# A two-layer graph network on one core: separate banks for two products, a range check kept per batch, a norm's sum from VectorE, and new orders

## The chip, the cores and the metric

The kernel runs on one core of a Trainium2 chip. The core has five engines with a queue each: TensorE (PE in the profile, with its weight loads shown apart as PEld) multiplies matrices, VectorE (DVE), ScalarE (ACT) and GpSimd (POOL) work on elements, and SyncE (SP) issues DMAs. TensorE writes into PSUM, which has eight banks here (`"ps": 8`); everything else lives in SBUF or in DRAM. An engine runs its queue in order; waits between engines go over semaphores. The metric is the device time of one execution in microseconds, the median of several runs; lower is better.

## The reference

`x` has 64 batches of 256 tokens with 512 features. Each batch goes through two layers, both with the same 256 x 256 adjacency `adj`, and each layer ends in a residual and a layer norm.

```python
# layer 0: attention with 8 heads of 64, masked by adj
q, k, v = x @ Wq + bq, x @ Wk + bk, x @ Wv + bv          # split into heads
scores = einsum('bqhd,bkhd->bhqk', q, k) / sqrt(64) + (1 - adj) * -1e9
x = layernorm(x + einsum('bhqk,bkhd->bqhd', softmax(scores), v) @ Wo + bo)
# layer 1: attention with one head from two scalars per token
h = x @ W
e = leaky_relu((h @ a1)[:, :, None] + (h @ a2)[:, None, :], 0.2) * adj
x = layernorm(x + elu(softmax(e) @ h + beta * h))
```

## The kernel before

**Products.** Every large product of layer 0 and layer 1 is done by a scheme of seven products in place of eight (`project`, L436): both factors are cut into quarters, sums of quarters are made beforehand (`weight_sums`, `streamed`, `token_sums`), and seven products of quarters are added up to the four quarters of the result. Product 1, 6 and 7 accumulate in one bank (`ps_chain`), 5 and 3 in another (`ps_cross`); between them their values are read out: `copy` starts a quarter of the result, `add` adds to it. Product 2 and 4 are the second and the fourth. Where the result is 256 wide (q, k, v, done for two batches at once) they have banks of their own (`ps_second`, `ps_fourth`); where it is 128 wide (`width == P`: spread, o, u) they share the two halves of one bank (`ps_pair`), and product 4 is recorded with `[second]` as something that it waits for (L480). ScalarE copies and VectorE adds (`gather`, L487); for o, VectorE adds all parts into X (L943).

**Stages of a pair of batches.** The kernel takes the batches two by two (`pair`, L616). "x" brings the pair in transposed; "q", "k" and "v" project it. Then for each batch (0 or 1, the digit behind a stage's name): "scores" in four calls of two heads, with keys on the partitions (matmuls of tile shape 64*128, two at a time); VectorE adds the mask (L783), ScalarE takes the exponential (L785), GpSimd adds the two halves (L788), VectorE transposes and reduces them to partial sums (L794, L795). "sums" folds these with one small matmul into `ps_den` (128*64), VectorE takes the reciprocal `inv` (L806), and two steps of DMA spread it over the partitions (L810, L814). "mix" multiplies the exponentials with v (`ps_pv`, 128*64); ScalarE copies, VectorE multiplies by the spread reciprocals (L867). "o" projects onto the residual X. `norm` (L581) then takes the sum of a token on ScalarE (L588, first pass), the mean on VectorE (L594), the squares on ScalarE (L588, second pass), the inverse root on GpSimd (L599 to L601), and scales on ScalarE (L605). "logits" and "attention" make layer 1's softmax from two scalars per token (L968) and two round trips over DRAM; "spread" multiplies it with X (`yT`), "u" multiplies by W. `finish` (L712) takes the exponential on ScalarE (L716), adds the positive part and then the rest on VectorE (L717, L719), calls `norm` again and stores.

**Order.** No engine's order is written by hand except TensorE's, in outline. `ROUND` lists the stages of one round; `LATER` says how many rounds after its own pair a stage is done, so that a round holds stages of several pairs; `FINISH` lists the closing stages. `Plan` (L62) records all operations with estimated durations and places them: TensorE in the order of the turns, the last 70 turns freely (`OPEN`), the other engines by due times worked back from TensorE, and with the slots of each pool as limits. In a round of before, TensorE does v, spread1, o1, q, u1, sums0, mix0, the scores of one batch, k, spread0, o0, u0, sums1, mix1 and the scores of the other batch (x, logits and attention have no matmul here).

**The range check.** The fast path is right if all reciprocals of the softmax sums lie between 1e-15 and 1e15. They are all kept in a DRAM tile `rows_all`; at the end it is read back (L1121) and compared as a whole (`check`, L1125). For the last batch `last_ok` does it apart. If the check fails, the program does everything again in a slower, general way.

Of the kernel before, what the change touches and what calls it, by code (L numbers as in the profile page):

```python
# [12 lines left out]
ALU = mybir.AluOpType  # L13
AX = mybir.AxisListType
PSUM = bass.MemoryType.PSUM

P = 128
# [2 lines left out]
ALPHA = 0.2  # L20
NEG = -1000000000.0

ROUND = ("scores20", "x", "scores10", "v", "logits0", "spread1", "o1", "q", "u1", "sums0", "mix0", "scores11",
         "scores01", "attention0", "attention1", "scores31", "scores21", "k", "logits1", "spread0", "o0", "u0",
         "sums1", "mix1", "scores00", "scores30")

LATER = {"mix1": 0, "sums1": 0, "scores30": -1, "scores20": 0, "scores00": -1, "scores10": 0, "logits0": 1, "v": 0,
         "spread1": 2, "o1": 1, "u1": 2, "x": -1, "mix0": 0, "sums0": 0, "scores31": 0, "scores21": 0, "scores01": 0,
         "scores11": 0, "attention0": 1, "q": -1, "attention1": 1, "logits1": 1, "k": -1, "spread0": 1, "o0": 0, "u0":
         1}  # L30

FINISH = (("logits0", 1), ("attention0", 1), ("scores20", 0), ("v", 0), ("spread1", 2), ("scores10", 0), ("o1", 1),
          ("scores21", 0), ("sums0", 0), ("u1", 2), ("mix0", 0), ("logits1", 1), ("attention1", 1), ("spread0", 1),
          ("u0", 1), ("scores11", 0), ("scores31", 0), ("o0", 0), ("u1", 1), ("sums1", 0), ("attention1", 0),
          ("attention0", 0), ("logits0", 0), ("spread1", 1), ("mix1", 0), ("o1", 0), ("u0", 0), ("logits1", 0),
          ("scores01", 0), ("u1", 0), ("spread1", 0), ("spread0", 0))
SAFE = 1e15


# [204 lines left out]
def gnn_two_layers(ctx: ExitStack, tc: tile.TileContext, x, adj, Wq, bq, Wk, bk, Wv, bv, Wo, bo, W, a, beta, out):  # L244
# [11 lines left out]


    slots = {"xin": 2, "x": 4, "two": 6, "xP": 1, "piece": 6, "full": 4, "half": 17, "flip": 1, "part": 1, "inv": 1,
             "xS": 2, "st": 76, "ps": 8, "rows": 4, "svT": 4, "line": 4, "square": 4}

    class Pool:

# [18 lines left out]
    def st(n, name):  # L281
        return sb("st", [n], name)
# [57 lines left out]
    ones = const.tile([P, 48], F32, name="ones")  # L340
    nc.gpsimd.memset(ones, 0.0)
    nc.gpsimd.memset(ones[:, 16:32], 1.0)
    rows_all = Buf(dram_pool, "rows_all", [B - 1, H * N], "rows_all")
    slots["rows_all"] = plan.slots["rows_all"] = 1
    stay.append(rows_all)
    last_ok = st(1, "last_ok")
    fold_sb = once([32], "fold_sb")
    plan.op("DVE", 150, lambda: nc.vector.tensor_reduce(
# [87 lines left out]
    def project(left, right, by_feature, claims, copy, add, inner=2, width=P, first=False):  # L436

        shape = [2, width] if by_feature else [width // P, F]
        chain, cross = ps(shape, "ps_chain"), ps(shape, "ps_cross")
        if width == P:
            both = ps([2] + shape, "ps_pair")
            second, fourth = (both, 0), (both, 1)
        else:
            second, fourth = (ps(shape, "ps_second"), None), (ps(shape, "ps_fourth"), None)

        def product(n, dst, start):  # L450
            l, r = sides[n][0](), right[n - 1][0]()
            for f in range(2 if by_feature else width // P):
                for c in range(inner):
                    lhs, rhs = (l[:, c, blk(f)], r[:, c, :]) if by_feature else (r[:, c, blk(f)], l[:, c, :])
                    nc.tensor.matmul(dst[:, f, :], lhs, rhs, start=start and f == 0 and c == 0, stop=c == inner - 1,  # L455
                                     skip_group_check=True)

        ns = 224 * inner * 2 if by_feature and width == P else 432 * inner * (width // P)

        sides = {}  # L460

        def pe(n, to, start, after=()):
            buf, part = to
            acc = (lambda: buf[A]) if part is None else (lambda: buf[:, part])
            sides[n] = left(n) if callable(left) else left[n - 1]
            plan.op("PE", ns, lambda: product(n, acc(), start), sides[n][1] + right[n - 1][1] + list(after),
                    [to] + list(after), claims=claims)
            return to, acc

        chain, cross = (chain, None), (cross, None)  # L470
        copy((0, 0), pe(1, chain, True))
        if first:
            add((0, 0), pe(2, second, True))
        copy((1, 1), pe(5, cross, True))
        if not first:
            add((0, 0), pe(2, second, True))
        copy((0, 1), pe(6, chain, False))
        if not first:
            add((0, 1), pe(3, cross, False))
        copy((1, 0), pe(4, fourth, True) if second[1] is None else pe(4, fourth, False, [second]))  # L480
        if first:
            add((0, 1), pe(3, cross, False))
        acc = pe(7, chain, False)
        add((1, 1), acc)
        add((1, 0), acc)
# [92 lines left out]
    for sv in spare:  # L578
        plan.op("POOL", 100, lambda sv=sv: nc.gpsimd.memset(sv[A], 0.0), [], [sv])

    def norm(X, ts):  # L581

        n = len(ts)
        sums, mean, sq, rs, nm = (st(n, name) for name in ("sum", "mean", "sq", "rs", "nmr"))

        def total(i, t, func, to, bias):
            junk = sb("half", [D], "junk")
# [1 line left out]
                junk[A], X[:, t, :], func, bias=mean[:, i:i + 1] if bias else 0.0, accum_out=to[:, i:i + 1]),  # L589
                [(X, (t, 0)), (X, (t, 1))] + ([mean] if bias else []), [junk, (to, i)])  # L590

        for i, t in enumerate(ts):
            total(i, t, AF.Identity, sums, False)
        plan.op("DVE", 170, lambda: nc.vector.tensor_scalar(mean[A], sums[A], -1.0 / D, None, ALU.mult), [sums], [mean])  # L594
        for i, t in enumerate(ts):
# [103 lines left out]
    def batch(m, s, qT, kT, V, dram, general):  # L699
# [11 lines left out]

        def finish(ts, us, u, mode):  # L712

            for t in ts:
                m = sb("half", [D], "m")
                plan.op("ACT", 620, lambda t=t, m=m: nc.scalar.activation(m[A], u(t), AF.Exp), us(t), [m])  # L716
                plan.op("DVE", 685, lambda t=t: nc.vector.scalar_tensor_tensor(  # L717
                    X[:, t, :], u(t), 0.0, X[:, t, :], op0=ALU.max, op1=ALU.add), us(t), tokens(t), mode=mode)
                plan.op("DVE", 685, lambda t=t, m=m: nc.vector.scalar_tensor_tensor(  # L719
                    X[:, t, :], m[A], 1.0, X[:, t, :], op0=ALU.min, op1=ALU.add), [m], tokens(t), mode="two")  # L720
            norm(X, ts)
            for t in ts:
                plan.op("SP", 455, lambda t=t: nc.sync.dma_start(dram(out, s)[:, t, :], X[:, t, :]), tokens(t), [],
                        lag=2300)
# [35 lines left out]
        def attention_by_keys():  # L760
# [38 lines left out]
            def denominators():  # L799

                turn("sums")
                acc, inv = ps([32], "ps_den"), sb("inv", [32], "inv")
                plan.op("PE", 80, lambda: nc.tensor.matmul(  # L803
                    acc[0:P // 2], part[A].rearrange("p h q -> p (h q)"), fold_sb[A], start=True,
                    stop=True), [part, fold_sb], [acc], mode="one", claims=[inv])
                plan.op("DVE", 342, lambda: nc.vector.reciprocal(inv[0:P // 2], acc[0:P // 2]), [acc], [inv])  # L806
                spread_rows(lambda r: r.rearrange("(p q) -> p q", q=32), lambda: inv[0:H * N // 32], inv)

            def spread_rows(to, src, inv):
                plan.op("SP", 540, lambda: nc.sync.dma_start(to(rows_all[b]), src()), [inv], [(rows_all, b)], lag=1700)  # L810
                for i in range(2):
                    def spread(i=i):
                        r = rows_all[b]
                        nc.sync.dma_start(everywhere[i * HD:(i + 1) * HD], bass.AP(  # L814
                            tensor=r.tensor, offset=r.offset + i * N, ap=[[0, HD], [2 * N, C], [1, N]]))

                    plan.op("SP", 660, spread, [(rows_all, b)], [(everywhere, i)], lag=4700)

            def denominators_last():
                turn("sums")  # L820
# [290 lines left out]

    plan.turn = (B // 2 + 2, 0)
    fine, row, least = st(2, "fine"), ps([P], "row"), st(1, "least")
    kept, ok = sb("full", [C, N], "kept"), sb("full", [C, N], "ok")
    n = (B - 1) * H * N // P
    assert n <= C * N

    def flat(t):
        return t[A].rearrange("p c n -> p (c n)")[:, 0:n]

    plan.op("SP", 1000, lambda: nc.sync.dma_start(  # L1121
        flat(kept), bass.AP(tensor=rows_all[A].tensor, offset=rows_all[A].offset, ap=[[n, P], [1, n]])), [rows_all],
        [kept])

    def check():  # L1125
        nc.vector.tensor_scalar(flat(ok), flat(kept), SAFE, None, ALU.is_le)
        nc.vector.tensor_scalar(flat(kept), flat(kept), 1.0 / SAFE, None, ALU.is_ge)
        nc.vector.tensor_tensor(flat(ok), flat(ok), flat(kept), ALU.mult)
        nc.vector.tensor_reduce(fine[:, 0:1], flat(ok), AX.X, ALU.min)
        nc.vector.tensor_tensor(fine[:, 1:2], fine[:, 0:1], last_ok[A], ALU.mult)  # L1130

    plan.op("DVE", 4000, check, [kept, last_ok], [ok, kept, fine], mode="two")
    plan.op("PE", 110, lambda: nc.tensor.transpose(row[A], fine[:, 1:2].to_broadcast([P, P]), ident), [fine], [row],
            claims=[least])
    plan.op("DVE", 300, lambda: nc.vector.tensor_reduce(least[A], row[A], AX.X, ALU.min), [row], [least])
# [50 lines left out]
```

## Time and profile before

| What | Value |
|---|---|
| Median of 3 runs | 2680.02 us |
| Lowest and highest | 2679.56, 2680.05 us |
| Profiled execution | 2677.89 us |
| Its span, first to last instruction | 2676.1 us |
| Granted TensorE clock in it | 0.998 |
| One round in the steady part (two batches) | 82.4 us |
| TensorE busy in a round (1277.0 to 1359.4 us) | 82.27 us |
| VectorE, GpSimd, ScalarE busy in it | 66.04, 51.21, 46.02 us |
| DMA share in it | 0.42 |

The busy lines give for each engine its busy time, its share of the span and its number of instructions. In the timeline each line is a run of like instructions of one engine: start, length, engine, line of the kernel, operation, output and inputs with the tile shape and the size, the number of records; in brackets how long the engine stood idle before it and what ended that. One float32 matmul leaves two records. The ends of matmuls are modelled, so that lengths overlap the start of the next. "L788" is line 788 of the kernel.

### The profile page before, as it was taken

Reading aid. Unit: us, or ns where it says so; the run is one execution under the profiler, and the core shown is the slowest. Engines: PE = TensorE matmul, PEld = TensorE weight load, DVE = VectorE, ACT = ScalarE, POOL = GpSimd, SP = SyncE. Lnnn points to the kernel's source line nnn. Section 1 sums busy time; section 2 is a strip of 40 time slices with the busy share of each in tenths; the row PEclk is TensorE's granted clock in tenths of the full one; section 3 lists DMA queues with packets and bytes.
Section 4 is the critical chain, followed back from the end, with each engine's and each line's share of the span. In section 5 each row is a group of like instructions: output and inputs, shape, how many; then the busy total and the mean of one; then the engine's idle time right before and its main releaser. Section 6 shows DMA issues by size and latency. Waiting matters only on the chain.

```text
span 2676.1 us, 45973 instructions
## 1 busy us (share of the span) xinstructions
PE 2650.1 (99%) x15037; PEld 2314.3 (86%) x15037; DVE 2127.7 (80%) x4188; ACT 1476.8 (55%) x3457; POOL 1649.8 (62%) x2254
## 2 busy tenths in 40 slices
PE   9999999999999999999999999999999999999997
PEld 7888888888888888888888888888888888888885
DVE  6788787887888877878778788788887787877886
ACT  3456555555465564655655555556556465565566
POOL 5665565755656656666556575565765666655654
PEclk9999999999999999999999999999999999999999
DMA  8344353443444444434434344344444443443321
GB/s 249 96 102 123 104 131 94 115 119 106 123 105 115 107 114 114 123 97 111 123 106 132 91 118 119 107 123 104 116 108 112 116 120 100 111 123 105 93 75 52
DMA packets 583228, 301.21 MB, mean 113 GB/s; under 512 B 409416, under 2 KB 513864, under 8 KB 582984
## 3 DMA queue, kind: packets, MB, share of 16 engines
q1 hardware_dynamic: 582856, 298.20, 42.4%
q8 instruction: 123, 2.02, 0.3%
q14 instruction: 121, 0.99, 0.1%
q0 software_dynamic: 128, 0.01, 0.0%
HBM read 245.63 MB, written 52.48 MB: 111 GB/s over the span
## 4 chain that ended last, share of the span: by engine, by line
PE 98%; DVE 1%; ACT 0%; issue 0%; DMA 0%; POOL 0%; SPq 0%; ACTq 0%; DVEq 0%; POOLq 0%
PE ps_chain L455 34%; PE ps_cross L455 22%; PE ps_pair L455 11%; PE ps_sc L776 9%; PE ps_pv L753 8%; PE ps_second L455 6%; PE ps_fourth L455 6%; PE ps_den L803 0%; PE ps_plain L520 0%; DMA wq_sb<-in_L_gnn_Wq_dram 0%; DVE junk L968 0%; ACT junk L588 0%; PE ps_plain L515 0%; PE ps_y L1052 0%; PE ps_plain L517 0%
## 5 line engine op out<-in xcount | busy, mean ns | idle before, releaser
L788 POOL TENSOR_TENSOR both<-pT 128x256 f32<-128x256 f32 x504 | 381.3, 772 | 40.7 <-ACT pT L785 39.2
L588 ACT ACTIVATE junk<-x 128x512 f32<-128x512 f32 x256 | 159.7, 624 | 434.7 <-DVE x L945 426.6
L599 POOL TENSOR_SCALAR rs<-sq 128x2 f32<-128x2 f32 (+1 forms) x130 | 25.3, 195 | 538.1 <-ACT junk L588 535.0
L783 DVE TENSOR_TENSOR pT<-ps_sc,maskT_sb 128x512 f32<-128x512 f32 x512 | 316.6, 677 | 26.5 <-PE ps_sc L776 26.2
L785 ACT ACTIVATE pT<-pT 128x512 f32<-128x512 f32 x512 | 296.3, 621 | 21.2 <-DVE pT L783 20.9
L753 PE MATMUL ps_pv<-pT,v 128*64 128x256 f32 x2048 | 241.1, 382 | 0.0
L776 PE MATMUL ps_sc<-qT,kT 64*128 64x256 f32 x2048 | 239.4, 383 | 0.4 <-DVE kT L501 0.4
L968 DVE SCALAR_TENSOR_TENSOR junk<-x,wa_sb 128x512 f32<-128x512 f32 x256 | 231.9, 931 | 1.9 <-ACT x L605 1.8
L776 PEld LDWEIGHTS ps_sc<-qT,kT 64*128 64x128 f32 x2048 | 192.8, 187 | 46.0 <-issue 25.3
L605 ACT ACTIVATE x<-x,nmr,rs 128x512 f32<-128x512 f32 x256 | 201.0, 809 | 40.0 <-POOL nmr L601 38.2
L1077 POOL TENSOR_TENSOR X_sums<-x 128x256 f32<-128x256 f32 x126 | 135.7, 1092 | 128.3 <-DVE x L719 85.2
L753 PEld LDWEIGHTS ps_pv<-pT,v 128*64 128x64 f32 x2048 | 210.0, 137 | 2.7 <-issue 0.7
L794 DVE STREAM_TRANSPOSE flip<-both 128x512 f32<-128x512 f32 x252 | 176.2, 699 | 31.5 <-POOL both L788 28.1
L588 ACT ACTIVATE junk<-x,mean 128x512 f32<-128x512 f32 x256 | 183.0, 716 | 4.3 <-DVE mean L594 3.2
L795 DVE TENSOR_REDUCE part<-flip 128x16 f32<-128x512 f32 x252 | 170.0, 674 | 3.2
L737 POOL TENSOR_TENSOR x<-x,res_sb 128x512 f32<-128x512 f32 x128 | 160.8, 1279 | 0.0
L1006 POOL TENSOR_TENSOR e<-e,adj_sb 128x512 f32<-128x512 f32 (+1 forms) x66 | 81.9, 1241 | 99.0 <-DVE e L1003 99.0
L426 POOL TENSOR_TENSOR yS<-yT 128x256 f32<-128x256 f32 x126 | 92.1, 731 | 66.8 <-DVE yT L501 62.0
L455 PE MATMUL ps_chain<-so_sb,oS 128*128 128x256 f32 x504 | 129.4, 379 | 0.0
L455 PE MATMUL ps_chain<-sw_sb,yS 128*128 128x256 f32 x504 | 129.3, 379 | 0.0
L945 DVE TENSOR_TENSOR x<-x,ps_chain 128x256 f32<-128x256 f32 x252 | 99.6, 415 | 29.3 <-PE ps_chain L455 26.0
L455 PE MATMUL ps_chain<-sv_sb,xS 128*128 128x256 f32 x512 | 120.9, 379 | 0.0
(248 smaller groups left out, 7023.4 us busy)
## 6 DMA issues: line engine op xcount, KB each, us to landing
x<-in_x_dram SPq DMA_DIRECT2D x64, 512.0 KB, 3.7
out_dram<-x SPq DMA_DIRECT2D x128, 256.0 KB, 2.8
inv_all<-rows_all SPq DMA_DIRECT2D x126, 256.0 KB, 4.1
xin<-in_x_dram SPq DMA_DIRECT2D x248, 128.0 KB, 3.2
wq_sums<-wq_sums SPq DMA_DIRECT2D x124, 256.0 KB, 2.7
wk_sums<-wk_sums SPq DMA_DIRECT2D x124, 256.0 KB, 2.8
wq_sums<-in_L_gnn_Wq_dram SPq DMA_DIRECT2D x93, 256.0 KB, 3.1
wk_sums<-in_L_gnn_Wk_dram SPq DMA_DIRECT2D x93, 256.0 KB, 2.9
```

Source lines behind the costliest of these rows:

```text
L455: nc.tensor.matmul(dst[:, f, :], lhs, rhs, start=start and f == 0 and c == 0, stop=c == inner - 1, skip_group_check=True)
L588: plan.op("ACT", 815 if bias else 725, lambda: nc.scalar.activation(junk[A], X[:, t, :], func, bias=mean[:, i:i + 1] if bias else 0.0, acc ...
L605: plan.op("ACT", 810, lambda i=i, t=t: nc.scalar.activation(X[:, t, :], X[:, t, :], AF.Identity, bias=nm[:, i:i + 1], scale=rs[:, i:i + 1] ...
L737: plan.op("POOL", 1300, lambda t=t: nc.gpsimd.tensor_tensor(X[:, t, :], X[:, t, :], res_sb[A], ALU.add), [res_sb], tokens(t))
L753: nc.tensor.matmul(acc[r * HD:(r + 1) * HD, i, :], V[:, 2 * k + s, h * HD:(h + 1) * HD], pT[h][:, k, :], start=k == 0, stop=k == NT - 1)
L776: nc.tensor.matmul(acc[j][:, k, :], kT[r:r + HD, c, key_blk(k)], own(qT, r, c), start=True, stop=True)
L783: plan.op("DVE", 680, lambda h=h, i=i: nc.vector.tensor_add(pT[h][A], acc[i][A], maskT_sb[A]), [acc[i], maskT_sb], [pT[h]])
L785: plan.op("ACT", 620, lambda h=h: nc.scalar.activation(pT[h][A], pT[h][A], AF.Exp, scale=1.0 / HD ** 0.5), [pT[h]], [pT[h]])
L788: plan.op("POOL", 735, lambda h=h, i=i: nc.gpsimd.tensor_tensor(both[c][:, i, :], pT[h][:, 0, :], pT[h][:, 1, :], ALU.add), [pT[h]], [(bot ...
L794: plan.op("DVE", 700, lambda: nc.vector.transpose(turned[A], both[c][A]), [both[c]], [turned])
L795: plan.op("DVE", 685, lambda: nc.vector.tensor_reduce(part[:, 2 * c:2 * c + 2, :], turned[A].rearrange("p i (q k) -> p i q k", k=32), AX.X ...
L968: plan.op("DVE", 770, lambda t=t, i=i, junk=junk: nc.vector.scalar_tensor_tensor(junk[A], X[:, t, :], 1.0, wa_sb[:, i, :], op0=ALU.mult, o ...
```

## The change

Four things are done, and the orders are new.

- In `project`, second and fourth product of a spread (by feature, 128 wide) get banks of their own; o and u keep the shared one. The order of a spread's products becomes 1, 5, 2, 6, 4, 3, 7 (before: 1, 5, 2, 6, 3, 4, 7).
- `rows_all` goes. Each batch's reciprocals are compared when they are there, with two VectorE operations into a tile `fine_sb`; the DRAM tile for the spreading becomes a small one with four places in turn. The closing check reduces `fine_sb`.
- In `finish` VectorE's last addition also writes out its sum over the token, and `norm` takes that in place of ScalarE's first pass.
- `ROUND` and `FINISH` are new lists; in `LATER` scores00 and scores30 go from -1 to 0 and logits0 from 1 to 0. The pool of small tiles (`st`) has 72 places in place of 76.

```diff
-ROUND = ("scores20", "x", "scores10", "v", "logits0", "spread1", "o1", "q", "u1", "sums0", "mix0", "scores11",
-         "scores01", "attention0", "attention1", "scores31", "scores21", "k", "logits1", "spread0", "o0", "u0",
-         "sums1", "mix1", "scores00", "scores30")
+ROUND = ("x", "v", "spread1", "scores20", "scores10", "scores30", "scores00", "o1", "q", "logits1", "u1", "sums0",
+         "mix0", "scores11", "scores21", "scores01", "scores31", "attention0", "k", "spread0", "o0", "mix1",
+         "logits0", "sums1", "u0", "attention1")
...
-    rows_all = Buf(dram_pool, "rows_all", [B - 1, H * N], "rows_all")
-    slots["rows_all"] = plan.slots["rows_all"] = 1
-    stay.append(rows_all)
+    fine_sb = once([32], "fine_sb")
+    plan.op("POOL", 100, lambda: nc.gpsimd.memset(fine_sb[A], 1.0), [], [fine_sb])
...
-        if width == P:
+        small = by_feature and width == P
+        if width == P and not small:
             both = ps([2] + shape, "ps_pair")
             second, fourth = (both, 0), (both, 1)
         else:
...
+        def last_quarter():
+            copy((1, 0), pe(4, fourth, True) if second[1] is None else pe(4, fourth, False, [second]))
+
...
         copy((0, 1), pe(6, chain, False))
-        if not first:
-            add((0, 1), pe(3, cross, False))
-        copy((1, 0), pe(4, fourth, True) if second[1] is None else pe(4, fourth, False, [second]))
-        if first:
-            add((0, 1), pe(3, cross, False))
+        if first or small:
+            last_quarter()
+        add((0, 1), pe(3, cross, False))
+        if not first and not small:
+            last_quarter()
         acc = pe(7, chain, False)
...
-    def norm(X, ts):
+    def norm(X, ts, given=None):
...
-        for i, t in enumerate(ts):
+        for i, t in enumerate(ts if given is None else ()):
             total(i, t, AF.Identity, sums, False)
...
+            sums = st(len(ts), "sum")
...
-                plan.op("DVE", 685, lambda t=t, m=m: nc.vector.scalar_tensor_tensor(
-                    X[:, t, :], m[A], 1.0, X[:, t, :], op0=ALU.min, op1=ALU.add), [m], tokens(t), mode="two")
-            norm(X, ts)
+                plan.op("DVE", 770, lambda t=t, m=m: nc.vector.scalar_tensor_tensor(
+                    X[:, t, :], m[A], 1.0, X[:, t, :], op0=ALU.min, op1=ALU.add,
+                    accum_out=sums[:, t - ts[0]:t - ts[0] + 1]), [m], tokens(t) + [(sums, t - ts[0])], mode="two")
+            norm(X, ts, sums)
...
-                spread_rows(lambda r: r.rearrange("(p q) -> p q", q=32), lambda: inv[0:H * N // 32], inv)
...
+                for limit, op in ((SAFE, ALU.is_le), (1.0 / SAFE, ALU.is_ge)):
+                    plan.op("DVE", 180, lambda limit=limit, op=op: nc.vector.scalar_tensor_tensor(
+                        fine_sb[0:P // 2], inv[0:P // 2], limit, fine_sb[0:P // 2], op0=op, op1=ALU.mult),
+                        [inv, fine_sb], [fine_sb], mode="two")
+                rows = Buf(dram_pool, "rows", [H, N], "rows")
...
     def check():
-        nc.vector.tensor_scalar(flat(ok), flat(kept), SAFE, None, ALU.is_le)
-        nc.vector.tensor_scalar(flat(kept), flat(kept), 1.0 / SAFE, None, ALU.is_ge)
-        nc.vector.tensor_tensor(flat(ok), flat(ok), flat(kept), ALU.mult)
-        nc.vector.tensor_reduce(fine[:, 0:1], flat(ok), AX.X, ALU.min)
+        nc.vector.tensor_reduce(fine[:, 0:1], fine_sb[A], AX.X, ALU.min)
         nc.vector.tensor_tensor(fine[:, 1:2], fine[:, 0:1], last_ok[A], ALU.mult)
```

Placed by the planner, TensorE's round after the change is: v, spread1, the scores of one batch, o1, q, u1, sums0, mix0, the scores of the other batch, k, spread0, o0, mix1, sums1, u0. At the start, the first pair's scores come behind v and not between k and v. VectorE's queue behind the lone scores is six mask additions, then an addition of o1, a mask addition, an addition of o1, the last mask addition, and the rest of o1 between transposes and reductions. In the closing part, the four L968 of the last batch but one stand ahead of the last batch's reciprocal.

## The prediction

> **What bounds the kernel now.** I read the page's busy table and chain of waits first, then the timeline of TensorE in one steady round, then VectorE in the same microseconds, and last the few places where the closing sequence shows a change of TensorE's tile shape alone. The page:
>
> ```profile
> PE 2650.1 (99%) x15037; PEld 2314.3 (86%) x15037; DVE 2127.7 (80%) x4188; ACT 1476.8 (55%) x3457; POOL 1649.8 (62%) x2254
> ```
>
> TensorE is the bound, and the chain gives it 98%. But 99% busy is not the whole story: a matmul's recorded length includes a tail that overlaps its successor, so a short stop between two matmuls is filled by the tail and appears in no idle column. The Trainium skill says as much ("Trainium Kernel Development and Optimization", Best Practices: judge by other measures than matmul busy share). I therefore measure from start to start. TensorE in one round, around the first spread:
>
> ```profile
> 1304.11 0.61 PE L455 MATMUL ps_chain<-attT,x 128*128 128x128 f32 x4
> ...
> 1305.90 0.61 PE L455 MATMUL ps_cross<-attT,X_sums 128*128 128x128 f32 x4
> 1306.64 0.68 PE L455 MATMUL ps_pair<-att_sums,x 128*128 128x128 f32 x4
> 1307.16 0.61 PE L455 MATMUL ps_chain<-att_sums,X_sums 128*128 128x128 f32 x4
> 1307.60 1.03 PE L455 MATMUL ps_chain<-wo_sb,oT 128*128 128x256 f32 x4
> ```
>
> A product of four records lasts 0.45 us from its start to the next start; cross lasts 0.74 and the following pair 0.52. The spread takes 1307.60 - 1304.11 = 3.49 us, where seven products of 0.448 make 3.14: 0.35 us lost. The round's other spread (1339.35 to 1342.68 in the same view) loses 0.19. The reason is on VectorE:
>
> ```profile
> 1305.48 0.68 DVE L501 TENSOR_TENSOR kT<-ps_chain,kT 128x512 f32<-128x512 f32 x1
> 1306.08 0.41 DVE L501 TENSOR_TENSOR yT<-ps_pair,yT 128x256 f32<-128x256 f32 x1
> 1306.41 0.68 DVE L501 TENSOR_TENSOR kT<-ps_chain,kT 128x512 f32<-128x512 f32 x1
> ```
>
> Product four writes the bank in which VectorE still reads product two. That read stands behind an addition of the k projection, ends at 1306.49, and pair starts at 1306.64. Now the tile shapes (128*128 for most, 64*128 for scores, 128*64 for mix and denominators). A steady stretch, then scores alone, denominators behind scores, and mix with none:
>
> ```profile
> 1318.83 1.02 PE L455 MATMUL ps_chain<-sw_sb,yS 128*128 128x256 f32 x4
> 1323.50 3.72 PE L776 MATMUL ps_sc<-qT,kT 64*128 64x256 f32 x32
> 1328.98 1.89 PE L455 MATMUL ps_cross<-wv_sb,xT 128*128 128x256 f32 x8
> ...
> 2577.14 0.61 PE L455 MATMUL ps_chain<-att_sums,X_sums 128*128 128x128 f32 x4
> 2577.68 1.14 PE L776 MATMUL ps_sc<-qT,kT 64*128 64x256 f32 x8
> 2578.74 1.13 PE L455 MATMUL ps_chain<-wo_sb,oT 128*128 128x256 f32 x4
> 2579.71 1.03 PE L455 MATMUL ps_cross<-wo_sb,oT 128*128 128x256 f32 x4
> ...
> 2586.05 0.30 PE L803 MATMUL ps_den<-fold_sb,part 128*64 128x32 f32 x2
> 2586.28 1.13 PE L455 MATMUL ps_chain<-w_sb,yT 128*128 128x256 f32 x4
> ...
> 2591.56 1.03 PE L455 MATMUL ps_chain<-sw_sb,yS 128*128 128x256 f32 x4
> 2592.52 3.67 PE L753 MATMUL ps_pv<-pT,v 128*64 128x256 f32 x32
> 2596.12 2.86 PE L776 MATMUL ps_sc<-qT,kT 64*128 64x256 f32 x24
> ```
>
> With 0.216 us a record of full shape (0.112 at 128 columns) and 0.108 for scores and mix, the first stretch holds 9.50 us of work in 10.15: denominators, mix, scores and return lose 0.65. Scores alone hold 2.18 in 2.57: 0.39 lost. Mix loses 4.56 - 4.32 = 0.24 up to its own end, and the first full record after a return runs 0.10 late (1.13 against 1.03), so mix alone costs 0.34. Denominators behind scores add 0.23.
>
> **What the skill says.** "TensorEngine Tiling (Array Packing)", Key Properties: changing the tiling mode drains TensorE; the trace agrees, about 0.2 us a change. "PSUM — Partial Sum Buffer", PSUM bank collisions raise a hardware error: guard PSUM by bank and not by address; the wait of pair for a reader of the bank's other half is that guard. "VectorE: DVE Perf Modes", Two Vector instructions with no wait between them: an operation that writes out its accumulator is two instructions; the trace agrees (a DVE_READ_ACCUMULATOR of 77 ns beside each L968).
>
> **The change part by part.**
>
> 1. *Banks of their own.* Product four no longer waits for VectorE. Saved: (0.35 + 0.19) x 30 rounds = 16.2 us. Next in line is the last product, which waits for ScalarE's copy of the fourth-placed one (chain<-att_sums): that copy ended at 1306.47, and without the stop the last product would start at 1306.79, 0.32 later. Cross now has one product more ahead of it. The fourth bank is the price: the spread holds four of eight.
>
> 2. *The new order, steady part.* Before, a round has denominators-mix-scores twice: 2 x 0.65 = 1.30. After, scores of one batch stand alone behind the second spread (0.39), the other batch keeps its 0.65, and mix stands alone before the second u with its denominators behind it: 0.34 plus theirs. These have mix's tile shape, so no change lies between; no trace shows that place. Below: nothing, if they run beside mix's end; above: 0.23, as behind scores. I take 0.14, the 0.23 less the 0.09 by which an exit exceeds a record. Sum 1.52, so 0.22 more a round (0.08 to 0.31); 31 rounds: +6.8 us (+2.5 to +9.6).
>
> 3. *Does the new order make waits?* Scores behind the spread use the spread's own banks for their third and fourth pair, and o follows at once, with VectorE behind. The first mask addition comes 1.17 us after scores start (1323.50 to 1324.67); eight at a pitch of 0.60 and three additions of o at 0.34 end at 7.0. O's sixth product, due at 3.65 + 0.10 + 5 x 0.864 = 8.07, waits for the last of these: 1 us to spare. Ahead of that, VectorE has about 10 us of work between the second u and v's last additions (four x additions 2.4, two xT transposes 2.4, attT 0.7, two oT products 1.8, v 1.2, z and e 1.2), in 12 us. The first scores of a round are followed by 24 us (o, q, u), the second by 21 (k, spread, o) before mix. Denominators to o keep 25 us against two DMAs of 1.7 and 4.1. I cost new waits at nothing; if VectorE comes over 1 us late, each further 0.1 us costs up to 3 us.
>
> 4. *Second norm.* L588's first pass (630 + 186 ns, 128 times) leaves ScalarE: some 100 us of an engine 55% busy, hidden behind TensorE except for the last token tile. There the sum runs 2666.18 to 2666.88 and the squares start only at 2667.49; mean could be out by 2665.9: -1.5 us (-2 to -0.5). VectorE's L719 (679) gains an accumulator: nothing to +0.23 us, as L968 (909 median) is slower; at most 0.9 us a round, beside TensorE.
>
> 5. *Range check per batch.* Two operations of 64x32 on VectorE for each of 63 batches. The nearest row is the reciprocal of the same shape, 340 ns at a pitch of 0.26: 126 x 0.15 to 0.26 = 19 to 33 us of VectorE over the kernel, hidden; uncovered, up to 1 us a round. One DMA and the big check near the end go; they ran behind TensorE. SyncE issues the same two kinds of DMA per batch as before, now behind the round's new places, and each has the 25 us of point 3. The smaller pool of small tiles, the four places for rows in DRAM and the order of heads within a batch I cost at nothing: no wait in the view names them.
>
> 6. *Head.* Scores now follow v. Gone: the stop of the first scores for kT (35.35 to 36.89 for work of 0.86: 0.68) and the stop of the second q for GpSimd's sums (53.13 to 56.47 for 1.73: 1.6), since v, which those sums wait for, ends 4 us earlier while q still comes after scores. One detour of tile shape less (0.39). I take -2.5 (-3 to +1).
>
> 7. *Tail.* The waits view has TensorE waiting 2.3 us for L968 (tr_s), 0.4 for oT, 0.2 twice. The new closing order puts these four L968 ahead of the last reciprocal; later waits can replace them: -1.8 (-3.5 to +3).
>
> Sum: -16.2 + 6.8 - 2.5 - 1.8 - 1.5 = -15.2 us. The profiled execution took 2677.89 (span 2676.1): 2662.7. The median shown is 2680.02, 2.1 above; against it 2664.8.
>
> **Rivals.** *Half the gain goes to VectorE's queue* behind the lone scores: 0.3 us a round, 31 x 0.3 = 9: 2674. For it: VectorE is 80% busy, L968 stretches to 1.7 us. Against: no TensorE stop but the pair in the rounds before. *VectorE enters the scores late* and o's chain and the scores' last banks stop TensorE every round: it decides from 15.2/31 = 0.5 us a round; at 1 us it is +31: 2696, slower. For it: the added checks and accumulators all fall on VectorE, just before these scores. Against: point 3's spare 2 us plus 1. *The pair's wait only moves* to the last product, for ScalarE's copy: 16.2 comes back, 2681. Against: the 0.32 us counted above; and nothing else stands in ScalarE's order between these copies.
>
> **Numbers.** Forecast 0.70, half gain 0.12, late VectorE 0.11, moved wait 0.07. What a measurement tells from no change is 0.2%, 5.4 us. Faster: 0.70 + 0.11 = 0.81; within: 0.08; slower: 0.11. The likeliest case spans 2657 to 2672 with the ends of points 2, 4, 6 and 7; for 8 in 10 I reach to the half gain and a little past: 2656 to 2677.
>
> **What would show it.** Cross and fourth of a spread at 0.45 us start to start; a round of 82.1 us instead of 82.4; lone scores losing 0.39; denominators behind mix adding 0.1 to 0.2; no stop in the first 60 us beyond the loads; the squares of the last norm right behind its mean. A stop before scores' third pair, or before o's fourth or sixth product, would prove me wrong.

## The result, and the profile after

| Kernel | Median | Lowest and highest | Against before (95% interval) |
|---|---|---|---|
| before, beside it | 2679.79 us | 2679.29 to 2680.05 | |
| after | 2713.89 us | 2713.24 to 2716.73 | 1.013 (1.0112 to 1.0147) |

The change made the kernel 34 us slower where 15 us less was forecast. The profiled execution took 2716.73 us (span 2714.9), the longest of the four. The busy line and the chain of waits on the page of the changed kernel:

```profile
PE 2650.2 (98%) x15037; PEld 2283.0 (84%) x15037; DVE 2256.1 (83%) x4439; ACT 1427.2 (53%) x3201; POOL 1663.8 (61%) x2255
PE 87%; DVE 9%; ACT 3%; issue 1%; DMA 0%; POOL 0%; SPq 0%; DVEq 0%; POOLq 0%; ACTq 0%
```

TensorE is busy for as long as before (2650.1), but its share of the chain falls from 98% to 87%, and VectorE has 9%. VectorE's busy time grew by 128 us, of which 75 us (112.0 against 37.2) are in one line, the mean of a norm. The view of TensorE's waits has one that comes again and again, where the view of before has nothing:

```profile
PE ps_cross L455 <- ACT qT L498: 43.0, 29, 1.8
```

43 us in 29 waits, at most one a round; measured from start to start, as in the prediction, 1.6 us each. TensorE's timeline around one of them, changed kernel; the spread of that round stands first:

```profile
1353.81 0.61 PE L455 MATMUL ps_second<-attT,x 128*128 128x128 f32 x4
1354.26 0.61 PE L455 MATMUL ps_chain<-att_sums,X_sums 128*128 128x128 f32 x4
1354.71 0.61 PE L455 MATMUL ps_fourth<-att_sums,x 128*128 128x128 f32 x4
...
1371.12 1.89 PE L455 MATMUL ps_chain<-xS,wq_sums 128*128 128x256 f32 x8
1374.46 1.99 PE L455 MATMUL ps_cross<-xT,wq_sums 128*128 128x256 f32 x8 [1.45 <-ACT qT L498]
```

The spread runs at 0.45 us a product from start to start: its stop is gone. But q's product three, in place of 1.73 us after its predecessor, comes 3.34 us after it: 1.61 us lost for ScalarE's copy of the cross bank, and the product behind it runs 0.10 late (1374.46 to 1376.29). ScalarE and VectorE in the same microseconds, changed kernel:

```profile
1368.28 0.82 ACT L498 ACTIVATE qT<-ps_chain,bq_sb 128x256 f32<-128x256 f32 x2
1372.17 0.72 ACT L592 ACTIVATE junk<-x,mean 128x512 f32<-128x512 f32 x1 [3.08 <-DVE mean L598]
1372.89 0.45 ACT L498 ACTIVATE qT<-ps_cross,bq_sb 128x256 f32<-128x256 f32 x1
1373.25 0.71 ACT L592 ACTIVATE junk<-x,mean 128x512 f32<-128x512 f32 x1
1373.95 0.46 ACT L498 ACTIVATE qT<-ps_cross,bq_sb 128x256 f32<-128x256 f32 x1
```

```profile
1368.94 3.19 DVE L598 TENSOR_SCALAR mean<-sum 128x2 f32<-128x2 f32 x1
1372.05 0.68 DVE L801 TENSOR_REDUCE part<-flip 128x16 f32<-128x512 f32 x1
```

The copies of q's cross product (done on TensorE by about 1369.6) stand behind o1's squares in ScalarE's queue; the squares wait for the mean; and the mean, a VectorE operation on two elements, takes 3.19 us. GpSimd's timeline in the same microseconds says why:

```profile
1365.65 2.79 POOL L794 TENSOR_TENSOR both<-pT 128x256 f32<-128x256 f32 x4
1368.38 1.28 POOL L1015 TENSOR_TENSOR e<-e,adj_sb 128x512 f32<-128x512 f32 x1
1369.62 2.49 POOL L743 TENSOR_TENSOR x<-x,res_sb 128x512 f32<-128x512 f32 x2
```

GpSimd works without a gap here, through the additions of the lone scores (L794) and what had queued up behind them. When the mean starts, this run has lasted 15.8 us (1.7 us at the same mean in the kernel before); it ends at 1372.11, 0.02 us before the mean does. The Trainium skill ("SBUF — State Buffer", Who interferes with whom) says that a VectorE operation of the kind `tensor_scalar` can run in a mode that takes the SBUF port pair which VectorE shares with GpSimd, and that who comes second is held up in full; a `tensor_reduce` on trn2 never is. The trace agrees: the transposes and reductions beside the same run keep their 0.7 us, the mean does not. No view names the mode that an operation ran in; that the port is what the mean waits for is read from which operations are held up and beside what. The mean's durations (answers for one line, before and after):

```profile
L594 DVE TENSOR_SCALAR mean<-sum x130: 147/171/687, 95.6 to 2666.9; 128x2 f32<-128x2 f32 x126, 128x1 f32<-128x1 f32 x4
```

```profile
L598 DVE TENSOR_SCALAR mean<-sum x130: 152/170/3516, 93.8 to 2704.7; 128x2 f32<-128x2 f32 x126, 128x1 f32<-128x1 f32 x4
```

The three numbers are shortest, median and longest in ns. The median is the same; 29 of the 130, one for each of TensorE's 29 stops, now take 2.9 to 3.5 us. Before, 28 took 0.5 and 29 took 0.3: the mean already met the end of one GpSimd operation, and all of ScalarE's waits for it came to 3.2 us in the whole run.

### The profile page after: what moved, and what is told of

Same layout as the page of the kernel before. It is cut to its first block, busy times and chain, and to the rows that moved or that the text cites. A ratio compares the mean times of both kernels' runs of the same rounds, so it can differ in the third digit from the quotient of the medians.

```text
span 2714.9 us, 45841 instructions
## 1 busy us (share of the span) xinstructions
PE 2650.2 (98%) x15037; PEld 2283.0 (84%) x15037; DVE 2256.1 (83%) x4439; ACT 1427.2 (53%) x3201; POOL 1663.8 (61%) x2255
## 4 chain that ended last, share of the span: by engine, by line
PE 87%; DVE 9%; ACT 3%; issue 1%; DMA 0%; POOL 0%; SPq 0%; DVEq 0%; POOLq 0%; ACTq 0%
PE ps_chain L455 29%; PE ps_cross L455 21%; PE ps_sc L782 8%; PE ps_pv L759 8%; PE ps_fourth L455 7%; PE ps_pair L455 7%; PE ps_second L455 5%; DVE mean L598 3%; DVE flip L800 2%; ACT junk L592 2%; DVE part L801 1%; DVE x L954 1%; ACT qT L498 1%; DMA wq_sb<-in_L_gnn_Wq_dram 0%; PE ps_den L809 0%
## 5 line engine op out<-in xcount | busy, mean ns | idle before, releaser
L794 POOL TENSOR_TENSOR both<-pT 128x256 f32<-128x256 f32 x504 | 379.3, 776 | 11.0 <-ACT pT L791 11.0
L791 ACT ACTIVATE pT<-pT 128x512 f32<-128x512 f32 x512 | 309.9, 629 | 106.0 <-DVE pT L789 105.5
L789 DVE TENSOR_TENSOR pT<-ps_sc,maskT_sb 128x512 f32<-128x512 f32 x512 | 317.8, 682 | 13.6 <-PE ps_sc L782 11.6
L1086 POOL TENSOR_TENSOR X_sums<-x 128x256 f32<-128x256 f32 x126 | 126.3, 1018 | 256.2 <-DVE x L722 204.9
L977 DVE SCALAR_TENSOR_TENSOR junk<-x,wa_sb 128x512 f32<-128x512 f32 x256 | 225.1, 914 | 50.6 <-ACT x L609 49.6
L1015 POOL TENSOR_TENSOR e<-e,adj_sb 128x512 f32<-128x512 f32 (+1 forms) x66 | 82.6, 1252 | 290.0 <-DVE e L1012 287.6
L592 ACT ACTIVATE junk<-x 128x512 f32<-128x512 f32 x128 | 80.1, 626 | 322.9 <-DVE x L954 313.7
L759 PEld LDWEIGHTS ps_pv<-pT,v 128*64 128x64 f32 x2048 | 175.6, 137 | 44.6 <-issue 11.0
L603 POOL TENSOR_SCALAR rs<-sq 128x2 f32<-128x2 f32 (+1 forms) x130 | 34.8, 268 | 281.9 <-ACT junk L592 276.7
L455 PE MATMUL ps_cross<-xT,wq_sums 128*128 128x256 f32 x496 | 120.2, 385 | 43.0 <-ACT qT L498 43.0
L743 POOL TENSOR_TENSOR x<-x,res_sb 128x512 f32<-128x512 f32 x128 | 161.0, 1280 | 0.9 <-DMA x<-in_x_dram 0.9
L455 PEld LDWEIGHTS ps_cross<-xT,wq_sums 128*128 128x128 f32 x496 | 91.8, 190 | 65.9 <-ACT qT L498 54.6
L598 DVE TENSOR_SCALAR mean<-sum 128x2 f32<-128x2 f32 (+1 forms) x130 | 112.0, 862 | 34.8 <-ACT junk L592 34.6
L455 PE MATMUL ps_chain<-so_sb,oS 128*128 128x256 f32 x504 | 129.7, 380 | 0.0
```

Source lines behind the costliest of these rows:

```text
L592: plan.op("ACT", 815 if bias else 725, lambda: nc.scalar.activation(junk[A], X[:, t, :], func, bias=mean[:, i:i + 1] if bias else 0.0, acc ...
L759: nc.tensor.matmul(acc[r * HD:(r + 1) * HD, i, :], V[:, 2 * k + s, h * HD:(h + 1) * HD], pT[h][:, k, :], start=k == 0, stop=k == NT - 1)
L789: plan.op("DVE", 680, lambda h=h, i=i: nc.vector.tensor_add(pT[h][A], acc[i][A], maskT_sb[A]), [acc[i], maskT_sb], [pT[h]])
L791: plan.op("ACT", 620, lambda h=h: nc.scalar.activation(pT[h][A], pT[h][A], AF.Exp, scale=1.0 / HD ** 0.5), [pT[h]], [pT[h]])
L794: plan.op("POOL", 735, lambda h=h, i=i: nc.gpsimd.tensor_tensor(both[c][:, i, :], pT[h][:, 0, :], pT[h][:, 1, :], ALU.add), [pT[h]], [(bot ...
L977: plan.op("DVE", 770, lambda t=t, i=i, junk=junk: nc.vector.scalar_tensor_tensor(junk[A], X[:, t, :], 1.0, wa_sb[:, i, :], op0=ALU.mult, o ...
```

## The experiments

Times are medians; each run stood beside runs of the kernel before (2679.55 to 2680.25 us). For all kernels I also read three times off TensorE's timeline: the start of the first q that lies within a round, the length of a steady round (from q to q), and the time from the last such q to the end of the span. The first and the last of these q lie 29 rounds apart.

| Kernel | Median | Ratio (95% interval) | To the first q | Round | From the last q |
|---|---|---|---|---|---|
| before | 2679.79 | | 119.2 | 82.40 | 173.8 |
| after | 2713.89 | 1.013 (1.0112 to 1.0147) | 117.6 | 83.72 | 176.9 |
| e1, mean as a reduction | 2665.01 | 0.9942 (0.9926 to 0.9959) | 116.8 | 81.98 | 175.1 |
| e2, short residual | 2663.26 | 0.994 (0.9923 to 0.9957) | 116.7 | 81.98 | 172.9 |
| e3, orders alone | 2708.17 | 1.0105 (1.0088 to 1.0122) | 118.0 | 83.22 | 181.8 |
| e4, light VectorE | 2688.88 | 1.0034 (1.0021 to 1.0046) | 117.4 | 82.82 | 173.8 |
| e5, planner told | 2675.25 | 0.9982 (0.9975 to 0.9989) | 116.6 | 81.98 | 183.3 |
| e6, banks alone | 2666.47 | 0.9952 (0.9935 to 0.9968) | 119.9 | 81.82 | 178.2 |
| e7, edits in old orders | 2670.13 | 0.9964 (0.995 to 0.9978) | 119.4 | 81.82 | 181.9 |
| e8, the same, mean on ScalarE | 2663.81 | 0.994 (0.9924 to 0.9957) | 119.7 | 81.82 | 175.3 |
| e9, squares behind the copies | 2696.26 | 1.0062 (1.0046 to 1.0077) | 116.8 | 83.10 | 174.4 |
| e10, old rounds, new end | 2661.24 | 0.9929 (0.9915 to 0.9942) | 119.4 | 81.82 | 172.1 |

The theory: GpSimd's run holds up the mean, the mean holds up ScalarE's queue, and that queue holds up q. Rival A: VectorE has too much to do there, because of the added checks and accumulators. Rival B: squares ahead of copies in ScalarE's queue block q by themselves.

**e1: the mean in a form that doesn't take the shared port.** Every queue keeps its order.

```diff
             junk[A], X[:, t, :], func, bias=mean[:, i:i + 1] if bias else 0.0,
-            accum_out=to[:, i:i + 1]),
+            scale=1.0 if bias or given is not None else 1.0 / D, accum_out=to[:, i:i + 1]),
...
-        plan.op("DVE", 170, lambda: nc.vector.tensor_scalar(mean[A], sums[A], -1.0 / D, None, ALU.mult), [sums], [mean])
+        plan.op("DVE", 170, lambda: nc.vector.tensor_scalar(
+            mean[A], sums[A], -1.0 / D, None, ALU.mult) if given is not None else nc.vector.tensor_reduce(
+            mean[A], sums[A].unsqueeze(2), AX.X, ALU.add, negate=True), [sums], [mean])
```

> The changed kernel with one instruction in another form: the first norm's mean (L598) is made by a VectorE reduction over one element with a changed sign, and ScalarE's first pass scales by 1/512 beforehand. Every queue keeps its order. Theory (the small scaling of L598 waits for GpSimd's unbroken run of three SBUF operations, and ScalarE's queue stands behind it): L598 falls from 0.88 us on average to under 0.25, the stop of q's third product for ScalarE's qT copy (some 1.6 us a round, 48 us in all) goes, the time is 2666 us (2660 to 2672), below the kernel before. Rival A (VectorE's queue is too long there, from the added range checks and accumulators): L598 stands at the same place of the same queue, so nothing moves, 2714 us. Rival B (ScalarE's squares ahead of the qT copies are enough to block it, whenever the mean comes): at least half of the stop stays, 2690 us or more.

2665.01 us, 49 less than the changed kernel. VectorE and GpSimd of e1 at the same place of their queues, one view of each:

```profile
1343.49 0.11 DVE L600 TENSOR_REDUCE mean<-sum 128x2 f32<-128x2 f32 x1
```

```profile
1342.96 1.27 POOL L1018 TENSOR_TENSOR e<-e,adj_sb 128x512 f32<-128x512 f32 x1
1344.20 2.50 POOL L746 TENSOR_TENSOR x<-x,res_sb 128x512 f32<-128x512 f32 x2
```

The mean now runs in 0.11 us in the middle of GpSimd's operation. No q waits any more, though the squares still stand ahead of and between the copies, and VectorE has the same work. Rivals A and B fall as the cause of q's stop.

**e2: GpSimd's run made shorter instead.** Most of the residual bias is left out of X.

```diff
-            plan.op("POOL", 1300, lambda t=t: nc.gpsimd.tensor_tensor(X[:, t, :], X[:, t, :], res_sb[A], ALU.add),
+            plan.op("POOL", 1300, lambda t=t: nc.gpsimd.tensor_tensor(
+                X[:, t, 0:16], X[:, t, 0:16], res_sb[:, 0:16], ALU.add),
```

> The changed kernel, but GpSimd's two additions of the residual bias (L743) touch 16 of 512 columns, so most of that addition is left out; the planner's durations and every order stay. Theory: the run of GpSimd operations that holds up L598 ends some 2.3 us earlier, L598's long cases fall from 3.2 us to about 1, and with them the stop of q: 2667 us (2661 to 2676). Rival A (VectorE's queue) and rival B (ScalarE's order): 2714 and above 2690 us, L598 no shorter than 3 us.

2663.26 us, and 28 long means of 0.8 us in place of 3.2. VectorE and GpSimd of e2:

```profile
1343.46 0.81 DVE L598 TENSOR_SCALAR mean<-sum 128x2 f32<-128x2 f32 x1
```

```profile
1342.93 1.28 POOL L1016 TENSOR_TENSOR e<-e,adj_sb 128x512 f32<-128x512 f32 x1
1344.17 0.40 POOL L743 TENSOR_TENSOR x<-x,res_sb 128x16 f32<-128x16 f32 x2
```

The same instruction of VectorE, at the same place of its queue, follows what GpSimd does. With e1 this closes the first link from both sides: in this place the mean is late because of its form and because of what GpSimd does beside it.

**e3: the new orders alone, in the kernel before. e4: the changed kernel without the work added to VectorE** (no check per batch, the second norm's sum on ScalarE again).

```diff
-                    X[:, t, :], m[A], 1.0, X[:, t, :], op0=ALU.min, op1=ALU.add,
-                    accum_out=sums[:, t - ts[0]:t - ts[0] + 1]), [m], tokens(t) + [(sums, t - ts[0])], mode="two")
-            norm(X, ts, sums)
+                    X[:, t, :], m[A], 1.0, X[:, t, :], op0=ALU.min, op1=ALU.add), [m], tokens(t), mode="two")
+            norm(X, ts)
...
-                for limit, op in ((SAFE, ALU.is_le), (1.0 / SAFE, ALU.is_ge)):
...
-                        [inv, fine_sb], [fine_sb], mode="two")
```

> The kernel before with nothing but the three new lists (round, later, finish). Theory: the new place of o1 next to GpSimd's run is enough: the mean (L594) shows the long cases, q's stop is there in every round; the stops of the spreads stay too (16 us): 2728 us (2720 to 2736). Rival A (the added work on VectorE does it): no stop of q, only the detours of tile shape: 2683 us (2677 to 2688).

> The changed kernel without the checks per batch (nothing tests the reciprocals of any batch but the last) and with the second norm's sum on ScalarE as before; banks and orders stay as changed. Theory: the stop of q is still there: 2714 us (2708 to 2722). Rival A: VectorE has its old work again, the stop is gone: 2666 us (2660 to 2674).

2708.17 and 2688.88 us: both miss both theories' numbers, by 20 and 25 us on the low side of mine. The mean takes 2.8 to 2.9 us 29 times in both, so the new orders bring this about by themselves and rival A falls again. But q loses only 0.2 us (e3) and 0.3 us (e4) a round there. In these two the planner set one square, not two, ahead of the second half of the copy (ScalarE, e4):

```profile
1276.23 0.72 ACT L592 ACTIVATE junk<-x,mean 128x512 f32<-128x512 f32 x1 [1.81 <-DVE mean L598]
1276.86 0.19 ACT L592 ACTIVATION_READ_ACCUMULATOR junk<-x,mean 128x1 f32 x1
1276.95 0.46 ACT L498 ACTIVATE qT<-ps_cross,bq_sb 128x256 f32<-128x256 f32 x1
```

And a second wait appears, `ps_pair` of u for VectorE, 0.4 us a round in each: the late norm makes the scaled X late, L977 (L968 in e3, L971 in e4) waits for it on VectorE, and u's additions stand behind that. With the product behind each, which again runs late by up to 0.10, the two make up nearly all of the 0.84 us by which e4's round is longer than e1's. So the size of the loss hangs on where it comes out; I had carried over the 1.6 us of the changed kernel.

**e9: ScalarE's queue alone altered**, so that o1's squares stand behind both halves of the copy. It was run after the four below, to test this reading.

```diff
     order = plan.place()
+    order = behind(plan, order, squares, crossed)
```

(`behind` takes ScalarE's operations in their order, sets each first-norm square that stands up to four places ahead of the second cross copy of q just behind that copy, and merges the queues again.)

> The changed kernel with ScalarE's queue alone altered: in each round o1's two squares stand behind the two qT copies out of q's cross bank, not between them; the queues of the other engines are as they were. Theory: the mean still takes 3.2 us in 29 rounds, but q's stop for the qT copy goes, since it came through ScalarE's queue. What the late norm still delays is the scaled X, then L977 on VectorE, behind which u's additions stand: as in the run without the added VectorE work, u's second pair product may wait, here up to 1.05 us a round by the trace (the read of u's pair ends at 1383.36 us, the product would be due at 1382.45 without the stop of q). So between 2667 us (nothing comes out there) and 2698 us, likeliest 2685. If the stop of q does not come through ScalarE's order: 2714 us.

2696.26 us, at the upper end. The 29 means still take 3.2 us; the stop of q is gone; and TensorE's waits have a line for u in its place (L491 and L542 are L455 and L504 of the changed kernel):

```profile
PE ps_pair L491 <- DVE u L542: 25.6, 29, 1.0
```

By starts it is 1.04 us a round, against the bound of 1.05 worked out beforehand. ScalarE's order is the second link, and taking it away alone brings back about a third of the 49 us (17.6), since the delay leaves by the next door.

**e5: one word for the planner.** The mean is marked as an operation that shares GpSimd's port (`mode="two"`), which the planner knows how to place.

```diff
-        plan.op("DVE", 170, lambda: nc.vector.tensor_scalar(mean[A], sums[A], -1.0 / D, None, ALU.mult), [sums], [mean])
+        plan.op("DVE", 170, lambda: nc.vector.tensor_scalar(mean[A], sums[A], -1.0 / D, None, ALU.mult), [sums], [mean],
+                mode="two")
```

> The changed kernel with one word more: the operation that records the mean (L598) is marked as one that shares GpSimd's port (mode two), so that the planner places it, and what follows it, around GpSimd's run. The instruction itself is as in the changed kernel. By the recorded orders the first norm's squares then stand behind the qT copies on ScalarE. Theory: the mean no longer starts inside the run, its long cases are gone or cost nothing, q's stop is gone: 2665 us (2661 to 2670). If the form of the instruction, and not its place, is what costs, or if any other part of the new orders stops TensorE: 2690 us or more.

2675.25 us (2671.78 to 2676.16 in 20 runs). The steady part did as expected: 81.98 us a round as in e1, no mean of a round above 0.17 us. But the planner also made another closing part, 8.2 us longer than e1's, with waits for L978 (2.9 us) and for GpSimd's sums of attT (2.3 and 1.3 us). My number left that out.

**e6: the banks alone, in the kernel before. e7: banks, checks and second norm in the old orders. e8: e7 with the mean straight out of ScalarE's first pass.**

```diff
-        for i, t in enumerate(ts if given is None else ()):
-            total(i, t, AF.Identity, sums, False)
-        plan.op("DVE", 170, lambda: nc.vector.tensor_scalar(mean[A], sums[A], -1.0 / D, None, ALU.mult), [sums], [mean])
+        if given is None:
+            for i, t in enumerate(ts):
+                total(i, t, AF.Identity, mean, False)
```

(For e8, with `scale=1.0 if bias else -1.0 / D` in `total`; the second norm keeps its mean on VectorE.)

> The kernel before with nothing but the spread's banks and its order of products. Theory of the prediction (the stop of product four, 0.54 us a round, goes): 2680 - 16 = 2664 us (2660 to 2668). Rival (the pair's wait only moves to the last product, for ScalarE's copy): 2680 us. If the fourth bank is felt elsewhere, stops at other products show, and the time lies between.

> The changed kernel with the three old lists: banks, checks per batch and the second norm's sum, without the new orders. Theory: 16 us from the banks, 0.3 from the end, the added VectorE work hidden, the mean outside GpSimd's run: 2663 us (2659 to 2668). Rival A (the added work on VectorE costs by itself): 2675 us or more.

> As the run before, and the first norm's mean comes straight out of ScalarE's first pass (scaled by -1/512), so that VectorE has no part in it. In the old orders nothing waits for the mean: 2663 us, within 3 of the run before. If a wait for the mean still costs there: 5 us or more below it.

E6 came within its range, e7 2 us above. The round is the same 81.82 us in all three: 0.58 us less than before, and neither the checks nor the accumulators cost anything in it. E8 is 6.3 us below e7, which by my own words stood for a wait for the mean. In the rounds there is none; the difference is the closing part (181.9 against 175.3), where e7 waits 5.5 us with the transposes of the attention (`tr_a`) for VectorE and has another order altogether, so the expectation's test was too coarse to tell. Whether the mean has a part in that closing part was not tried. In e6 the closing part takes 4.4 us longer than in the kernel before and gives back a quarter of what the banks save.

**e10: a version to beat both.** As e1, with the old `ROUND` and `LATER` and the new `FINISH`.

```diff
-ROUND = ("x", "v", "spread1", "scores20", "scores10", "scores30", "scores00", "o1", "q", "logits1", "u1", "sums0",
+ROUND = ("scores20", "x", "scores10", "v", "logits0", "spread1", "o1", "q", "u1", "sums0", "mix0", "scores11",
...
-         "scores30": 0}
+         1}
```

> A version meant to beat both: banks, checks per batch and the second norm's sum as changed, the old lists for the round and for what is done later, the new closing list, and the first norm's mean as a reduction. Theory: rounds of 81.8 us as with the edits in the old orders, a mean that GpSimd can't hold up, and a closing part of 175 us or less where the old list had 182: 2661 us (2657 to 2667). If the new closing list brings nothing with the old rounds: 2668 us or more.

2661.24 us: 19.0 below the kernel before beside it, 52.7 below the changed one, and the lowest of all.

## Why the prediction was wrong

The step that failed is point 3, "I cost new waits at nothing". It asked whether VectorE comes in time to the scores' masks and o's additions, and for that it looked at the sum of VectorE's work. It didn't follow o1 one step further, into its norm: the mean on VectorE, in the middle of GpSimd's run that the lone scores had just filled, and the squares on ScalarE, between q's copies. The runs put 49 us in the place of that nothing (after less e1). That o1's norm stands beside these GpSimd operations was to be seen in the profile of before; how long it would be held was not, since there the same two L737 follow and the mean took only 0.3 us (last section). The rival "VectorE enters the scores late" foresaw a slower kernel, but at another place and for another cause: in the rounds neither the scores' third pair nor o's products stop, and in the round above the masks keep the times of point 3 (the first 1.17 us after the scores start, the last done after 6.8).

All else of the sum can be read from e1, which is the changed kernel without that wait: it took 2665.01 us where 2664.8 was forecast. That closeness is partly luck. From first to last q, e1 is 11.6 us shorter than before, where points 1 and 2 together made 9.4; its end is 1.3 us longer, where points 4 and 7 made 3.3 shorter; and in the profiled spans it gains 12.7 us, by medians 14.8 (the profiled execution of before was 2 us shorter than its median). The terms:

- *Point 1, banks:* right. 0.54 us a round was predicted; e6's rounds are 0.58 shorter. The rival that the wait only moves falls: in the changed kernel no product of a spread stops.
- *Point 2, new order:* right in sign, a little too large. +0.22 a round was predicted; e1 less e7 is +0.16. The denominators behind mix, for which 0.14 was taken, add 0.09: from 1413.75 to 1419.36 the changed kernel has 5.18 us of work, and mix alone accounts for 0.34 of the 0.43 lost. The lone scores lose 0.39 as stated (1356.14 to 1359.79 for 3.46 us of work, and 0.10 in the product behind, and 0.09 ahead of them). The stretch with the denominators:

```profile
1413.75 1.03 PE L455 MATMUL ps_chain<-so_sb,oS 128*128 128x256 f32 x4
1414.70 3.67 PE L759 MATMUL ps_pv<-pT,v 128*64 128x256 f32 x32
1418.21 0.25 PE L809 MATMUL ps_den<-fold_sb,part 128*64 128x32 f32 x2
1418.39 1.13 PE L455 MATMUL ps_chain<-w_sb,yT 128*128 128x256 f32 x4
1419.36 1.03 PE L455 MATMUL ps_cross<-w_sb,yT 128*128 128x256 f32 x4
```

- *Points 4 and 5, VectorE's added work:* hidden, as stated: the rounds of e7, which has it, are as long as those of e6, which has not.
- *Point 4, last norm:* mis-sized. -1.5 us was predicted; from the end of TensorE's work to the end of the span it is 12.50 us before and 12.21 after, -0.3. The mean did come early, but the squares are not right behind it. ScalarE, changed kernel, at the end:

```profile
2703.83 2.21 ACT L609 ACTIVATE x<-x,nmr,rs 128x512 f32<-128x512 f32 x3
2705.94 0.71 ACT L592 ACTIVATE junk<-x,mean 128x512 f32<-128x512 f32 x1
```

The mean was out at 2704.85; three scalings of other tiles stand ahead of the square. It is the same oversight as in point 3: ScalarE's order was not looked at.

- *Point 6, head:* -2.5 predicted, -2.4 in e1 up to the first q (-1.6 in the profiled run after).
- *Point 7, tail:* -1.8 predicted, or -3.3 with the last norm. From the last q to the end it is +1.3 us in e1 and +3.0 after, of which 1.6 is one more stop of q. The waits for L968 went, but new ones of 1.7 us each came (for oT, and for the last batch's masks).

The parts of the profiled span add up: the 29 rounds between first and last q +37.3, head -1.6, closing part +3.0, together 38.7 of 2714.9 - 2676.1 = 38.8 us.

## What to carry to other kernels

When an order changes, follow each moved stage through every engine's queue down to its smallest operation: an operation on two elements can hold up TensorE if it stands in line for a resource that a neighbour keeps busy, and if an in-order queue stands behind it. A duration whose longest cases lie far above its median (0.69 against 0.17 us, in the profile of before) can point to such a resource, even while nobody waits. Give small operations a form or an engine that doesn't share the resource, and tell the planner of those that do; and judge steady rounds and closing part apart, since the closing part moved by 11 us between variants whose rounds were the same to 0.2 us.

## What the runs showed of the hardware that was not expected

The Trainium skill ("SBUF — State Buffer", Who interferes with whom) also says that who issues first has the pair for the whole instruction. Here the mean was held up past the instruction that was running when it started (that one ended 0.72 us later) and through the two that followed without a gap: 3.19 us in this round, 2.9 to 3.5 in all 29 cases of the changed kernel. In e4 it was likewise, 2.86 us up to the end of the run.

It need not be so. In the kernel before, the mean of o1 also starts inside a GpSimd addition behind which the same two L737 (L743 of the changed kernel) follow without a gap, and it is out some 0.02 us after the end of the first, in all 29 cases. VectorE and GpSimd, kernel before:

```profile
1268.90 0.33 DVE L594 TENSOR_SCALAR mean<-sum 128x2 f32<-128x2 f32 x1 [1.07 <-ACT junk L588]
```

```profile
1268.48 0.73 POOL L426 TENSOR_TENSOR yS<-yT,yS 128x256 f32<-128x256 f32 x1
1269.16 2.51 POOL L737 TENSOR_TENSOR x<-x,res_sb 128x512 f32<-128x512 f32 x2
```

In e7 it gets in between L1015 and an L743, both of 512 elements (0.9 us, 26 times), and in e2 between L1016 (512 elements) and two short operations. So neither the length of GpSimd's run nor the size of what follows decides alone whether VectorE gets its turn at the end of an operation. In the cases held to the end the mean stands right behind a VectorE transpose, and in the kernel before and e7 VectorE had been idle; but in e2 it stands behind the same transpose and gets in. What decides it was not tried and stays open.
